# Masked row maximum in the first attention layer: TensorE mask only in score banks of two or four heads

## The chip, the cores and the metric

The kernel runs on one core of one Trainium2 chip. The metric is the device time of one execution in microseconds. Three runs of the kernel before gave 665.36, 666.23 and 666.69, so the median is 666.23 us.

## The reference

The input `x` is four sequences of 512 tokens and 256 channels. Six residual blocks follow each other, each on a layer norm of `x`:

```
x = x + 0.5 * ffn0(ln(x))     # dequantised weights, silu gate, hidden size 704
x = x + attn0(ln(x))          # 16 heads of 16, rotary embedding, causal
x = x + 0.5 * ffn0(ln(x))
x = x + 0.5 * ffn1(ln(x))     # ternary weights found from mean |w|, sigmoid gate
x = x + attn1(ln(x))          # 16 query heads, 4 key heads, linear bias, causal
x = x + 0.5 * ffn1(ln(x))
```

An attention layer computes, for each head, `softmax(q k^T / 4 + causal mask) v`. The softmax needs, for each query row, the maximum of the row's scores over the keys that the mask leaves. The change touches only how that maximum is found, and only in `attn0`.

## The kernel before

**Layout.** L is the layer pair (0 or 1), b the sequence (0 to 3). One attention `attn(L, b)` handles its 16 heads in four groups `g` of four heads. Queries and keys of a group lie in `Qs[g]` and `Ks[g]`, split into bf16 parts along the partitions, and reach these tiles over DRAM (`parts` writes, `fill` in L487 to L495 reads back, all on the SP queue).

**Pass 1** (`pass1`, L574 to L614) finds the row maxima of a group. Queries are taken in four chunks `c` of 128 rows; because of the causal mask, chunk `c` needs only the first `128*(c+1)` keys. A `unit` fills one PSUM bank of 512 columns (tag `s`, four buffers, shared with pass 2 and with a few FFN tiles): chunk 0 puts four heads of 128 keys into one bank, chunk 1 two heads of 256 keys (two units), and chunks 2 and 3 one head of 384 or 512 keys (four units each). This makes 11 units for each group, eight of them with one head. In the trace the bank of a unit is called `s_<g><c><first head>a`, so `s_132a` is group 1, chunk 3, head 2.

There are two forms of a unit. In the form called `summed`, used for L = 0 and b < 2, TensorE adds the mask into the bank with one more matmul, identity times a 128x128 mask block (L591), repeated for each head; then VectorE takes the maximum of all heads of the bank with one `tensor_reduce` (L593). In the other form, used everywhere else, no mask matmul runs; VectorE adds the mask and takes the maximum in one `tensor_tensor_reduce` for each head (L597), which the trace shows as two instructions, a CUSTOM_DVE_ANT_0 that writes the masked scores back into the bank, and a DVE_READ_ACCUMULATOR2_ANT that delivers the maximum to `mxt`.

`fin` (L601) then transposes `mxt` on TensorE (L605), splits the negated maxima into two bf16 rows on VectorE (L607, L608) and sends these to two rows of `Qs[g]` over SP (L610).

**Pass 2** (`pass2`, L618) computes the scores again in transposed form with the maxima already subtracted (L639), takes the exponential on ScalarE (L644), zeroes the masked corner on GpSimd (L646), and multiplies by the values (L659).

**Other work beside it.** The FFNs (`mtile` L369, `down` L421, activation parts L391 to L410), layer norms (L315 to L350), projections (L467, L565, L749), rotary embedding (L519 to L524). While the first two sequences are in `attn0`, the weights of `ffn1` are loaded in pieces over SP, summed as absolute values on ScalarE (L190, L201), turned into a threshold (`level`, L205 to L213) and quantised on VectorE (L229, L230).

**What sets the order.** Every piece of work is a function with a due time in `plan`, made from the tables `PLAN` and `MOVES` (a correction for single entries of the list, by their number); the pieces are issued in the order of due time (`plan.sort`, L818). The kernel is then built with `schedule_with_timeline_sim=True` (L907): the framework places each engine's instructions by its own estimate of how long they take, with the issued order as priority. The order on an engine is fixed when the kernel is built; every engine then works strictly through its own list.

Of the kernel before, what the change touches and what calls it, by code (L numbers as in the profile page):

```python
# [84 lines left out]
def macaron(ctx, tc, x, gu0, wd0, s0, sd0, wa0, wq1, wkv1, wo1, bo1, gu1, wd1,  # L85
# [365 lines left out]
    def attn(L, b, tag):  # L451
# [119 lines left out]
        def kst(g):  # L571
            return Ks[g] if L == 0 else Ks[b % 2]

        def pass1(g):  # L574

            Q, K = Qs[g], kst(g)

            summed = L == 0 and b < 2

            def unit(c, hs, N):  # L580
                def f():
                    mx = mxt[g % 2][:, 0:16].rearrange("p (h c) -> p h c", h=4)
                    p = psc.tile([128, T], F32, tag="s", name=f"s1_{g}{c}{hs[0]}{tag}")
                    st = N
                    n = len(hs)
                    for i, h in enumerate(hs):
                        PE.matmul(p[:, i * st:i * st + N], Q[0:mr, h, c * 128:(c + 1) * 128],  # L587
                                  K[0:mr, h, 0:N], start=i == 0 or not summed, stop=not summed)
                    if summed:
                        pm = p[:, 0:n * N].rearrange("p (h n) -> p h n", n=N)  # L590
                        PE.matmul(pm[:, :, N - 128:N], identb, mask[:, T - 128:T].unsqueeze(1).to_broadcast([128, n, 128]),  # L591
                                  start=False, stop=True)
                        V.tensor_reduce(mx[:, hs[0]:hs[0] + n, c], pm, AX.X, ALU.max)  # L593
                        return
                    for i, h in enumerate(hs):
                        pi = p[:, i * st:i * st + N]
                        V.tensor_tensor_reduce(pi, pi, mask[:, T - N:T], 1.0, FLOOR, ALU.add, ALU.max,  # L597
                                               mx[:, h, c:c + 1])
                return f

            def fin():  # L601


                pt = pmm.tile([128, T], F32, tag="mm", name=f"mt{g}{tag}")
                PE.transpose(pt[:, 0:128], mxt[g % 2], ident)  # L605
                mt = wrk.tile([16, 2, 128], BF, tag="mt", name=f"mts{g}{tag}", bufs=1)
                V.tensor_scalar(mt[:, 0], pt[0:16, 0:128], -1.0, None, ALU.mult)  # L607
                V.scalar_tensor_tensor(mt[:, 1], pt[0:16, 0:128], -1.0, mt[:, 0], ALU.mult, ALU.subtract)  # L608
                for l in range(2):
                    SY.dma_start(Q[mr + l:mr + l + 1], mt[:, l])  # L610

            us = [unit(0, (0, 1, 2, 3), 128), unit(1, (0, 1), 256), unit(1, (2, 3), 256)]
            us += [unit(c, (h,), 128 * (c + 1)) for c in (2, 3) for h in range(4)]
            return us, fin  # L614

# [143 lines left out]
        if quick:  # L759
            pre = [list(th) + [rope(1, "k")], [rope(0, "q"), vproj(0), vproj(1)]]  # L760
        return dict(pre=pre, fills=fills, pass1=pass1, pass2=pass2,
                    post=([ctr(0)] if tail else []) + [ctr(1), oproj(0), oproj(1)], dram=None if tail else (fetch, recip, norm))

# [147 lines left out]
```

## Time and profile before

| quantity | value |
|---|---|
| median of three runs | 666.23 us (665.36 to 666.69) |
| the profiled execution, whole | 665.67 us |
| its span in the trace | 663.9 us, so 1.77 us lie around it |
| TensorE clock granted, mean | 0.995 |
| busy: TensorE matmul, VectorE, ScalarE, GpSimd | 635.8, 525.1, 450.6, 386.4 us |
| mask matmuls of L591 | 88, from 72.4 to 185.6 us |
| `tensor_reduce` of L593 | from 72.9 us to the last start at 188.65 us |

All times in the trace are in microseconds from the start of the span. PE is TensorE's matmuls, PEld its weight loads, which run beside them, DVE is VectorE, ACT ScalarE, POOL GpSimd, SPq the queue of SyncE that issues the DMAs. A line of a timeline gives start, duration, engine, line of the code, operation, tile written and tiles read. Durations of neighbouring instructions on one engine overlap in the trace, because an engine starts an instruction before the last one has left its pipeline. What an instruction takes from its engine is therefore the distance from its start to the next start, and not its duration.

### The profile page before, as it was taken

The numbers are of one execution on the slowest core, as the hardware profiler recorded it, in microseconds if no ns is written. First come the engines' busy times: TensorE is split into PE (matmuls) and PEld (weight loads), VectorE is DVE, ScalarE is ACT, GpSimd is POOL, SyncE is SP. The second block draws the span as 40 slices with busy tenths as digits, with TensorE's granted clock in tenths as the row PEclk, the third lists the DMA queues.
The fourth block names the chain that finished last, engine by engine and source line by source line (L and its number), as shares of the span: only waits on it lengthen the run. The fifth ranks groups of instructions, "written<-read, shape, count | busy, mean of one in ns | idle before, by whom it ended". The sixth has DMA issues, their size and how long they took to land.

```text
span 663.9 us, 13241 instructions
## 1 busy us (share of the span) xinstructions
PE 635.8 (96%) x4405; PEld 430.4 (65%) x4405; DVE 525.1 (79%) x1515; ACT 450.6 (68%) x893; POOL 386.4 (58%) x648
## 2 busy tenths in 40 slices
PE   7898899999989999999999999999999999999996
PEld 5686666556635776657676766776575674566585
DVE  7789889789799987887778797787969778895344
ACT  3675658777758477785859678685948757757733
POOL 4655957667528765576547756488645544543511
PEclk8999999999999999999999999999999999999999
DMA  8204504326551322222221221111311232101000
GB/s 273 94 2 135 150 2 137 106 77 203 166 166 52 96 70 72 81 63 82 81 63 29 77 67 51 35 37 51 98 58 29 74 92 74 53 3 33 0 33 33
DMA packets 38290, 51.41 MB, mean 77 GB/s; under 512 B 10634, under 2 KB 28458, under 8 KB 38222
## 3 DMA queue, kind: packets, MB, share of 16 engines
q1 hardware_dynamic: 37646, 49.85, 24.8%
q10 hardware_dynamic: 576, 0.72, 0.4%
q8 instruction: 35, 0.57, 0.4%
q14 instruction: 33, 0.27, 0.1%
HBM read 34.12 MB, written 16.16 MB: 76 GB/s over the span
## 4 chain that ended last, share of the span: by engine, by line
PE 75%; DVE 8%; ACT 7%; POOL 6%; issue 2%; DMA 1%; ACTq 0%; DVEq 0%; POOLq 0%
PE pf L369 22%; PE df L421 11%; PE o0a L659 3%; PE o1a L659 3%; PE o3a L659 2%; PE o2a L659 2%; PE po0a L749 2%; PE po1a L749 2%; PE ltf L347 2%; ACT xnf L343 1%; POOL X L753 1%; PE pv1a L565 1%; POOL hlf L407 1%; PE pv0a L565 1%; PE paqa L467 1%
## 5 line engine op out<-in xcount | busy, mean ns | idle before, releaser
L369 PE MATMUL pf<-xhf,GU 128*128 128x512 f32 x352 | 123.6, 439 | 6.6 <-ACT xhf L349 2.8
L407 POOL TENSOR_TENSOR hlf<-hf,hhf 128x512 fp32r<-128x512 f32 x72 | 94.5, 1313 | 44.8 <-ACT hhf L406 44.1
L369 PE MATMUL pf<-xlf,GU 128*128 128x512 f32 x352 | 110.2, 401 | 0.0
L369 PEld LDWEIGHTS pf<-xhf,GU 128*128 128x128 f32 x352 | 60.8, 192 | 32.5 <-ACT xhf L349 4.9
L587 PEld LDWEIGHTS <-Qs 96*128 96x128 bf16 (+1 forms) x512 | 43.9, 98 | 53.8 <-issue 40.9
L369 PEld LDWEIGHTS pf<-xlf,GU 128*128 128x128 f32 x352 | 66.4, 190 | 15.5 <-DVE xlf L350 0.2
L639 PEld LDWEIGHTS <-Ks 98*128 98x128 bf16 (+1 forms) x512 | 43.2, 98 | 42.5 <-issue 30.3
L406 ACT CAST hhf<-hf 128x512 fp32r<-128x512 f32 x80 | 49.7, 621 | 22.1 <-DVE hf L404 15.6
L421 PE MATMUL df<-WD,hhf 128*128 128x256 f32 x320 | 53.8, 286 | 2.3 <-ACT hhf L406 2.2
L404 DVE SCALAR_TENSOR_TENSOR hf<-tf,pf 128x512 f32<-128x512 f32 (+1 forms) x48 | 32.9, 685 | 27.7 <-PE pf L369 18.1
L597 DVE DVE_READ_ACCUMULATOR2_ANT mxt<- 128x1 f32 x384 | 52.7, 137 | 0.2
L421 PE MATMUL df<-WD,hlf 128*128 128x256 f32 x320 | 50.9, 285 | 0.0
L421 PEld LDWEIGHTS df<-WD,hhf 128*128 128x128 f32 x320 | 44.4, 188 | 4.6 <-ACT hhf L406 3.8
L399 POOL TENSOR_TENSOR hf<-tf,hf 128x512 f32<-128x512 f32 x30 | 39.5, 1315 | 10.5 <-DVE tf L396 5.4
L343 ACT ACTIVATE xnf<-X,mrf,rsf 128x256 f32<-128x256 f32 x60 | 31.8, 593 | 18.2 <-POOL mrf L323 10.7
L421 PEld LDWEIGHTS df<-WD,hlf 128*128 128x128 f32 x320 | 43.2, 189 | 0.5
L403 ACT ACTIVATE tf<-pf 128x512 f32<-128x512 f32 (+1 forms) x48 | 28.1, 595 | 14.2 <-PE pf L369 14.0
L646 POOL TENSOR_SCALAR_AFFINE_SELECT Ks<-Ks 128x128 f32<-128x128 f32 (+2 forms) x54 | 19.3, 357 | 25.9 <-ACT Ks L644 25.3
L395 ACT ACTIVATE tf<-pf,sgh 128x512 f32<-128x512 f32 (+1 forms) x36 | 24.9, 691 | 7.0 <-PE pf L369 6.6
L349 ACT CAST xhf<-ltf 128x512 fp32r<-128x512 f32 x32 | 18.4, 591 | 15.4 <-PE ltf L347 15.0
L396 DVE SCALAR_TENSOR_TENSOR tf<-tf,pf 128x512 f32<-128x512 f32 (+1 forms) x36 | 24.4, 679 | 5.1 <-ACT tf L395 4.8
L315 DVE BATCH_NORM_STATS2 bsf<-X 128x6 f32<-128x256 f32 x64 | 23.6, 413 | 3.5 <-POOL X L426 2.3
(700 smaller groups left out, 2042.5 us busy)
## 6 DMA issues: line engine op xcount, KB each, us to landing
Qs<-drqa SPq DMA_DIRECT2D x96, 128.0 KB
Ks<-drka SPq DMA_DIRECT2D x60, 128.0 KB
out_dram<-X SPq DMA_DIRECT2D x8, 256.0 KB
droa<-oT0a SPq DMA_DIRECT2D x7, 256.0 KB
droa<-oT1a SPq DMA_DIRECT2D x7, 256.0 KB
cna<-droa SPq DMA_DIRECT2D x7, 256.0 KB
X<-in_x_dram SPq DMA_DIRECT2D x3, 512.0 KB
drka<-raka SPq DMA_DIRECT2D x4, 384.0 KB
```

The costliest lines, as they stand in the source:

```text
L343: S.activation(xn[c], X[b][:, c], AF.Identity, bias=mr[:, i:i + 1], scale=rs[:, i:i + 1])
L369: PE.matmul(p, w[:, m:m + 128], xx[:, k], start=n == 0, stop=n == 3)
L399: G.tensor_tensor(h, t, h, ALU.mult)
L403: S.activation(t, g, AF.Tanh, scale=0.5)
L404: V.scalar_tensor_tensor(h, t, 1.0, u, ALU.add, ALU.mult)
L406: S.copy(hh, h)
L407: (V if big and i % 2 or (first or last and big) and i > 2 else G).tensor_tensor(hl, h, hh.bitcast(F32), ALU.subtract)
L421: PE.matmul(p[:, cc], ho[l, i][:, ts], WD[L][:, i], start=n == 0, stop=n == 10)
L587: PE.matmul(p[:, i * st:i * st + N], Q[0:mr, h, c * 128:(c + 1) * 128], K[0:mr, h, 0:N], start=i == 0 or not summed, stop=not summed)
L597: V.tensor_tensor_reduce(pi, pi, mask[:, T - N:T], 1.0, FLOOR, ALU.add, ALU.max, mx[:, h, c:c + 1])
L639: PE.matmul(p[:, i * N:i * N + N], K[0:nr, h, kc * 128:(kc + 1) * 128], Q[0:nr, h, kc * 128:T], start=True, stop=not steep(h))
L659: m = PE.matmul(o[0][32 * h:32 * h + 32, kc * 128:T], va[:, kc, hv * VS:hv * VS + 32], pt[kc, h], start=kc == 0, stop=kc == 3)
```

## The change

`summed` is no longer decided once for the attention, but for each unit, and the condition gains `c < 2`. For L = 0 and b < 2, the units of chunks 0 and 1 (four and two heads in the bank) keep the mask matmul and the common `tensor_reduce`; the units of chunks 2 and 3 (one head) take the other form. With eight such units in each of four groups of two sequences, 64 units change. Plan, due times and everything else stay as they are.

```diff
             Q, K = Qs[g], kst(g)
 
-            summed = L == 0 and b < 2
 
             def unit(c, hs, N):
+
+                summed = L == 0 and b < 2 and c < 2
+
                 def f():
                     mx = mxt[g % 2][:, 0:16].rearrange("p (h c) -> p h c", h=4)
```

## The prediction

> **What bounds the kernel now.** I read the page first, for the busy shares and the chain that ended last; then the busy time of each engine in windows over the stretch that the change touches (72 to 206 us); then the timelines of TensorE and VectorE there, start to start; last the waits.
>
> The page:
>
> ```profile
> span 663.9 us, 13241 instructions
> PE 635.8 (96%) x4405; PEld 430.4 (65%) x4405; DVE 525.1 (79%) x1515; ACT 450.6 (68%) x893; POOL 386.4 (58%) x648
> PE 75%; DVE 8%; ACT 7%; POOL 6%; issue 2%; DMA 1%; ACTq 0%; DVEq 0%; POOLq 0%
> ```
>
> TensorE is busy nearly always and holds three quarters of the chain; VectorE is second in both. So work taken from TensorE shortens the run wherever VectorE has room. The windows (columns: window, length, busy time and count of PE, PEld, DVE, ACT, POOL, then clock, DMA share, GB/s):
>
> ```profile
> 72.00:80.00 8.00, 7.97 (x58) 5.64 (x57) 7.13 (x13) 6.01 (x11) 7.84 (x11) 1.00 0.51 154
> 80.00:88.00 8.00, 7.49 (x60) 6.09 (x58) 7.09 (x15) 2.19 (x4) 4.13 (x4) 1.00 0.01 1
> 95.00:112.00 17.00, 17.00 (x125) 11.17 (x123) 16.57 (x29) 14.37 (x29) 13.09 (x20) 1.00 0.29 96
> 112.00:126.00 14.00, 13.88 (x99) 7.88 (x98) 9.05 (x18) 10.77 (x22) 10.38 (x18) 1.00 0.42 131
> 126.00:148.00 22.00, 21.90 (x158) 12.20 (x157) 18.52 (x33) 16.24 (x35) 13.24 (x27) 1.00 0.25 73
> 178.00:190.00 12.00, 10.11 (x82) 4.96 (x82) 11.86 (x30) 9.35 (x19) 5.38 (x14) 1.00 0.56 169
> ```
>
> Three kinds of stage are to be seen. From 72 to 88 VectorE sets the pace: in its timeline it runs from 72.87 to 86.0 without a gap, and GpSimd is full to 80. From 95 to 148 TensorE is full; VectorE is nearly full too up to 112 and has room after that. From 178 to 190 VectorE is full with quantising the ffn1 weights, while TensorE has 1.9 us idle. The timeline places the 64 units so: 16 from 73 to 88, 8 from 95 to 106, 8 from 107 to 121, 16 from 126 to 149, 8 from 155 to 173, 8 from 177 to 186.
>
> **What is removed: 64 mask matmuls on TensorE.** The record of one is 219 ns (L591, 128 columns), but its price is the start-to-start distance. The TensorE timeline, with two kinds of follower:
>
> ```profile
> 87.36 0.39 PE L587 MATMUL s_132a<-Ks,Qs 96*128 96x512 bf16 x1
> 87.59 0.22 PE L591 MATMUL s_132a<-mask,identb 128*128 128x128 bf16 x1
> 87.65 0.38 PE L587 MATMUL s_133a<-Ks,Qs 96*128 96x512 bf16 x1
> ...
> 105.40 0.22 PE L591 MATMUL s_233a<-mask,identb 128*128 128x128 bf16 x1
> 105.43 0.71 PE L369 MATMUL pf<-xhf,GU 128*128 128x512 f32 x2
> 105.98 0.63 PE L369 MATMUL pf<-xlf,GU 128*128 128x512 f32 x2
> ...
> 109.50 0.62 PE L369 MATMUL pf<-xhf,GU 128*128 128x512 f32 x2
> 109.96 0.63 PE L369 MATMUL pf<-xlf,GU 128*128 128x512 f32 x2
> ```
>
> Before another score matmul the mask takes 0.06 us (87.59 to 87.65). Before an fp32 matmul it takes 0.03, and the follower is then held back by its own 190 ns weight load: the pair at 105.43 takes 0.55 to its successor, the undisturbed pair at 109.50 takes 0.46, so 0.03 + 0.09 = 0.12. Eleven of the 64 are followed by an fp32 matmul of pf, df, po or paqa, the other 53 I put at 0.06 (some show more, up to 0.15 before the value product, where a wait lies in the distance). 53 x 0.06 + 11 x 0.12 = 3.2 + 1.3 = 4.5 us of TensorE, 0.07 for one unit.
>
> **What is replaced on VectorE: 64 reduces by 64 pairs.** The durations suggest a large loss: 546 ns (384 columns) and 679 ns (512) against 556 + 137 and 730 + 137. The VectorE timeline says otherwise:
>
> ```profile
> 76.66 0.68 DVE L593 TENSOR_REDUCE mxt<-s_030a 128x1 f32<-128x512 f32 x1
> 77.26 0.68 DVE L593 TENSOR_REDUCE mxt<-s_031a 128x1 f32<-128x512 f32 x1
> ...
> 205.16 0.73 DVE L597 CUSTOM_DVE_ANT_0 s_032a<-s_032a,mask 128x512 f32<-128x512 f32 x1
> 205.81 0.14 DVE L597 DVE_READ_ACCUMULATOR2_ANT mxt<- 128x1 f32 x1
> 205.81 0.68 DVE L396 SCALAR_TENSOR_TENSOR tf<-tf,pf 128x512 f32<-128x512 f32 x1
> 206.41 0.69 DVE L597 CUSTOM_DVE_ANT_0 s_033a<-s_033a,mask 128x512 f32<-128x512 f32 x1
> 207.01 0.14 DVE L597 DVE_READ_ACCUMULATOR2_ANT mxt<- 128x1 f32 x1
> ```
>
> A reduce holds VectorE 0.60 us. The masked maximum holds it 0.60 (206.41 to 207.01) when another kind of operation went before, and 0.65 (205.16 to 205.81) when an accumulator read did; the read starts together with what follows it and adds nothing more. Over the whole trace, wherever no wait comes between, the medians are 0.47 and 0.60 for the reduce, 0.48 and 0.61 for the pair, 0.515 and 0.65 after a read. So 0.01 to 0.05 more for one unit. I take 0.03, the middle, since runs of one-head units and mixed places are about equally common: 64 x 0.03 = 1.9 us (0.6 to 3.2).
>
> A rule of the Trainium skill speaks against this: "VectorE: DVE Perf Modes", section Rules for kernel authors, says to minimise the count of operations, since each pays its own pipeline drain. By it the 0.14 us of each read would be added whole, some 9 us of VectorE as an estimate, and the change would lose. The start-to-start rows above don't show that cost.
>
> **Waits and queues.** No DMA is added or moved, on SP or on any other queue. The VectorE instruction no longer waits for the mask matmul, so it may start 0.06 earlier. The bank is written back and comes free later: the CUSTOM lasts 0.69 to 0.73 against 0.68, and if the read's end counted it would be 0.14 more, so 0.01 to 0.19 per bank. In the stretch TensorE waited for a bank held by L593 four times, 0.2 to 0.3 each; four waits longer by these bounds cost 0.04 to 0.8 us, and behind such a wait stands everything else on TensorE's list. I take 0.2, near the row of the CUSTOM, which is the one that uses the bank. The last maximum of a group, which L605 and the SP transfers of L610 wait for, comes later by at most the same 0.19; behind L610 on SP stand the fills of L495 and the weight pieces of L190 and L221. That lies inside the same bound and I count it once.
>
> **The sum by stage.** From 72 to 88: TensorE's 16 x 0.07 = 1.1 us falls into waits for VectorE and GpSimd, so I count none of it; VectorE's 16 x 0.03 = 0.5 is partly swallowed by its gaps of 0.2 and 0.7 us at 86 and 87, so 0.2, and the bank waits lie here, 0.2 more: +0.4 (bounds -1.1 and +1.3). From 95 to 106: both are full, 8 x 0.07 = 0.56 on one side and nothing or 0.24 on the other, I take half: -0.3. From 107 to 121: -0.56. From 126 to 149: 16 x 0.07 = -1.1. From 155 to 173: -0.5, TensorE holds most of the chain there. From 177 to 186: VectorE holds the chain, 8 x 0.03: +0.2, and TensorE's saving falls into its idle time. Together -1.9, say -2 us. After 190 the code is the same and TensorE holds most of the chain, so the lead is carried to the end. The SP transfers of the ffn1 weights in between wait for buffers that the engines free and not for a clock of their own, so they move with the lead.
>
> One term has no row: the framework places instructions by its own estimates, so that 64 other instructions can change the order on every engine from 72 us on. The nearest row is the largest hole of TensorE here, 2.79 us idle between 185 and 195 (7.21 busy of 10); one such hole more or fewer bounds it at +2.8 and -2.8, two at +5.6. I take 0 in the sum, because the trace favours neither sign, and leave it to the range.
>
> The profiled execution took 665.67, so 663.7 by its own measure; it lies 0.56 under the median of 666.23. Against the median the forecast is 664.2 us, 0.3% faster.
>
> **The rivals.**
> *Another order costs more than is saved (slower).* One new hole of the size seen at 185 to 195, in a stretch where TensorE is full, less the 2 us: +0.8; two: +3.6, 669.8. It decides from one hole of 2 us upward. For it: units sit between FFN and pass 2 matmuls at fine grain (s_020a comes after s_032a at 77.44), so the order is open to small shifts. Against it: the two forms of the unit take the same time on VectorE, and the later sequences already run in the new form at 100% TensorE (245 to 265: 20.00 of 20.00). About 668.5.
> *VectorE pays the durations (slower).* If a pair costs 0.15 to 0.19 more, as durations say, 36 of the units stand where VectorE is full (16 + 8 before 106, about 4 up to 112, 8 after 177): 36 x 0.17 = 6.1, less 28 x 0.07 = 2.0: +4.1, 670.3. It decides from 0.06 a unit. Against it stand the start-to-start rows.
> *TensorE's saving is lost (no change).* The lead could end at 178 to 193, where the chain runs through VectorE and a weight DMA of 4.2 us, if that DMA is held by its own data: 666.2. The Trainium skill, "Trainium Kernel Development and Optimization", section Performance Expectations, calls matmul busy time a bad measure and the share of weight loads a good one; by that the 65% of PEld would leave TensorE room, and the sum would be near 0. The 95 to 148 rows show no gap, with fp32 matmuls back to back.
> *TensorE sets the pace everywhere.* All 4.5 us come out: 661.7. Against it, VectorE at 72 to 88 and 178 to 190.
>
> **How the numbers follow.** A measurement of this kernel tells about 0.2% (1.3 us) from no change. Chances: the forecast 0.32 (its own range 662.5 to 664.8), all of the saving 0.10, so faster 0.42; lost 0.18, the same; another order 0.30 and VectorE's durations 0.10, so slower 0.40. The range from 661 to 670.5 reaches from the full saving with a little over it to two holes and the durations' case; about 1 in 10 is left out at each end.
>
> **What would show it.** Right: mask matmuls 24 instead of 88; TensorE's busy time between 95 and 149 lower, the last L597 unit of b = 1 and the start of ffn1's quantising earlier by 1 to 2 us; the pair at 0.47 to 0.52 and 0.60 to 0.65 start to start between 72 and 190; the stage 72 to 88 as long as before or 0.4 longer. Wrong: VectorE's waits for banks grow, TensorE shows new idle stretches of over 1 us after 72, or the order of units against pf and df matmuls differs and the loss comes after 190, where no code changed.

## The result

The changed kernel takes 668.57 us (median of five, 668.08 to 669.07) beside 665.9 us for the kernel before: ratio 1.0033, 95% interval 1.0018 to 1.0049. A second measurement of the changed kernel gave 667.71 us and 1.0018 (1.0006 to 1.003). So it is slower by 0.2 to 0.3%, 1.2 to 2.2 us. The ratios here and below are those on record, with their intervals; they are not the quotients of the medians, which can lie 0.1% beside them (here 1.0040). The profiled execution took 668.57 us itself.

The page after:

```profile
span 666.6 us, 13180 instructions
PE 633.9 (95%) x4341; PEld 425.7 (64%) x4341; DVE 529.8 (79%) x1579; ACT 451.6 (68%) x893; POOL 386.4 (58%) x648
PE 73%; DVE 9%; ACT 7%; DMA 4%; POOL 4%; issue 2%; SPq 1%; ACTq 0%; DVEq 0%; POOLq 0%
```

The work did what was meant: TensorE has 64 matmuls fewer and is busy 1.9 us less, VectorE has 64 instructions more. The span is 2.7 us longer all the same. In the chain, DMA rose from 1 to 4% and TensorE fell from 75 to 73%. The windows (columns: window, length, busy time and count of PE, PEld, DVE, ACT, POOL, then clock, DMA share, GB/s):

```profile
72.00:80.00 8.00, 7.45 (x44) 4.75 (x43) 6.25 (x18) 6.58 (x12) 7.84 (x10) 1.00 0.65 184
80.00:88.00 8.00, 7.26 (x54) 5.88 (x53) 8.00 (x23) 2.37 (x5) 4.22 (x5) 1.00 0.00 0
95.00:112.00 17.00, 16.62 (x115) 10.57 (x114) 16.15 (x37) 13.93 (x29) 13.59 (x21) 1.00 0.24 77
112.00:126.00 14.00, 12.88 (x76) 6.98 (x74) 10.66 (x25) 10.18 (x20) 10.36 (x17) 1.00 0.44 145
126.00:148.00 22.00, 21.39 (x159) 11.51 (x157) 18.31 (x45) 16.04 (x35) 12.50 (x25) 1.00 0.27 78
178.00:190.00 12.00, 8.70 (x70) 3.85 (x69) 11.46 (x37) 9.62 (x22) 5.16 (x14) 1.00 0.47 145
```

TensorE, which was full from 95 to 148, now stands still for 0.38, 1.12 and 0.61 us in its three windows there, where it has 1.9 us less to do. This execution was already 1.14 us behind that of before at 60 to 72 us, where the code and the order are the same, so the fixed windows cover slightly different work. A better ruler is the start of the same TensorE instruction in both traces, the later one less the earlier one, less the value at 60 to 72 us; I call its median over a stretch the lag. For the changed kernel it is -0.22 us at 100 to 110, +0.89 at 114 to 121, +0.44 at 149 to 155, and +2.52 at 212 to 230; from there it falls slowly, to 1.6 at the end. So 1.1 us are lost in a few microseconds near 112, and about 2 more between 155 and 212, shortly before the point (216 us) from which both kernels run the same instructions in the same order.

Why there? When I compared the two programs, they did not only differ in the 64 units. Each engine's list is in another order too: between 77 and 216 us 54 instructions of TensorE stand at another place among the others, 38 of VectorE, 22 of ScalarE, 14 of GpSimd and 12 DMAs of SyncE. Before 77 us and after 216 us the lists agree. Here is one such difference, first before (start, duration, engine, line, operation):

```profile
110.64 0.69 DVE L410 TENSOR_TENSOR h5f<-hf,h5f 64x512 fp32r<-64x512 f32 x1
111.36 0.56 DVE L593 TENSOR_REDUCE mxt<-s_321a 128x1 f32<-128x384 f32 x1
...
111.50 1.17 POOL L484 TENSOR_TENSOR rcqa<-rq2a,rcqa 128x512 bf16<-128x512 f32 x1 [1.44 <-ACT rcqa L483]
112.62 0.30 POOL L646 TENSOR_SCALAR_AFFINE_SELECT P102a<-P102a 128x128 f32<-128x128 f32 x1
```

and then in the changed kernel (its lines from the unit on are numbered two higher):

```profile
111.94 0.57 DVE L599 CUSTOM_DVE_ANT_0 s_321a<-s_321a,mask 128x384 f32<-128x384 f32 x1 [0.35 <-PE s_321a L589]
...
112.60 1.50 DVE L410 TENSOR_TENSOR h5f<-hf,h5f 64x512 fp32r<-64x512 f32 x1
114.13 0.69 DVE L595 TENSOR_REDUCE mxt<-s_300a 128x4 f32<-128x512 f32 x1
...
112.39 1.17 POOL L484 TENSOR_TENSOR rcqa<-rq2a,rcqa 128x512 bf16<-128x512 f32 x1 [1.35 <-ACT rcqa L483]
113.51 0.75 POOL L648 TENSOR_SCALAR_AFFINE_SELECT P102a<-P102a 128x128 f32<-128x128 f32 x1
...
114.88 0.32 PE L589 MATMUL s_322a<-Ks,Qs 96*128 96x384 bf16 x1 [0.78 <-DVE mxt L595]
```

Two VectorE instructions have changed places. VectorE first waits 0.35 us for the bank s_321a, and `h5f` (the low part of an FFN activation) then starts just behind GpSimd's `rcqa` instead of ahead of it. The same instruction takes 1.50 us in place of 0.69, until GpSimd's is over; GpSimd's next one is drawn out too, from 0.30 to 0.75. The maximum of s_300a comes late, and TensorE waits 0.78 us for its bank, with the whole list behind. This is a *collision*: two instructions, neither of them changed, that happen to meet, so that one waits for the other.

### The profile page after: what moved, and what is told of

The parts are those of the page before. It is cut to its first block, busy times and chain, and to the rows that moved or that the text cites. A ratio compares the mean times of both kernels' runs of the same rounds, so it can differ in the third digit from the quotient of the medians.

```text
span 666.6 us, 13180 instructions
## 1 busy us (share of the span) xinstructions
PE 633.9 (95%) x4341; PEld 425.7 (64%) x4341; DVE 529.8 (79%) x1579; ACT 451.6 (68%) x893; POOL 386.4 (58%) x648
## 4 chain that ended last, share of the span: by engine, by line
PE 73%; DVE 9%; ACT 7%; DMA 4%; POOL 4%; issue 2%; SPq 1%; ACTq 0%; DVEq 0%; POOLq 0%
PE pf L369 20%; PE df L421 11%; PE o1a L661 3%; PE o3a L661 3%; PE o0a L661 2%; PE o2a L661 2%; PE po0a L751 2%; PE po1a L751 2%; PE ltf L347 1%; ACT xnf L343 1%; DMA ws<-in_gu_dram 1%; DMA wa0s<-in_wa_dram 1%; PE pv1a L565 1%; DVE tf L396 1%; PE pq1a L467 1%
## 5 line engine op out<-in xcount | busy, mean ns | idle before, releaser
L369 PE MATMUL pf<-xhf,GU 128*128 128x512 f32 x352 | 122.0, 433 | 7.1 <-ACT xhf L349 2.5
L599 DVE DVE_READ_ACCUMULATOR2_ANT mxt<- 128x1 f32 x448 | 62.2, 139 | 0.2
L398 ACT ACTIVATE hf<-pf,sgu 128x512 f32<-128x512 f32 x30 | 20.8, 694 | 9.2 <-PE pf L369 5.2
```

What stands on the lines that cost most here:

```text
L369: PE.matmul(p, w[:, m:m + 128], xx[:, k], start=n == 0, stop=n == 3)
```

## The experiments

**How an order is held fixed.** A kernel was built in which the framework may not choose: after all pieces are issued, each engine's instructions are chained by edges that cost no semaphore, in an order read from a table (`ORDER`).

```diff
+    marks = []
     for _, f in plan:
+        marks.append(len(nc.cur_bb.bb.instructions))
         f()
+    in_order(tc, nc, marks)
...
+def in_order(tc, nc, marks):
...
+    info = mybir.DependencyInfo(mybir.DependencyClass.NoSync, mybir.DependencyReason.SCHED_ONLY)
...
+            if last is not None:
+                tc.add_manual_dep(i, last.name, info, reason="order")
+            last = i
```

With before's instructions and before's own order this gives instruction for instruction the program of before, and with the changed kernel's instructions and order that of the changed kernel; so what is measured below is the order and not the edges. All kernels below but the last one have this edit; their further edit is shown with each. They keep the line numbers of before.

**Instructions and order, taken apart.** *New instructions, old order*: the change as in its diff, `ORDER` = before's. *Old instructions, new order*: before's `unit`, `ORDER` = the changed kernel's, each removed mask matmul put right behind its score matmul.

> The instructions of the changed kernel, but each engine's list held in the order that the kernel before has. Theory 'order' (the changed instructions save what the forecast said, and the loss comes from the new order on the engines): about 2 us under the kernel before, 663 to 665 us, and the mask matmuls 24 in number. Theory 'VectorE pays' (the masked maximum costs VectorE more than the reduce, so the order is beside the point): as slow as the changed kernel, 667.5 to 669.5. Theory 'start' (over 1 us of the loss is already there before 72 us, where no code changed): this run is at most 1 us away from the changed kernel less what the stretch after 72 us gave, so 667.

> The instructions of the kernel before (mask matmul and reduce in every bank of the first two sequences), in the order that the changed kernel has; each mask matmul stands right behind its score matmul. Theory 'order': slower than both, the changed kernel's 668.6 plus the 2 to 4.5 us that the mask matmuls take, 670 to 673. Theory 'VectorE pays': the order costs nothing, 665 to 667.

Measured: new instructions in the old order 666.04 beside 666.68 us, ratio **0.9982 (0.997 to 0.9994)**; old instructions in the new order 669.89 us, ratio **1.0056 (1.0037 to 1.0074)**. (The medians alone would give 0.9990 and 1.0048. The theory 'order' had expected 663 to 665 and 670 to 673 us, so both effects came out somewhat smaller than it said.) The instructions by themselves make the kernel faster by 0.18%, 1.2 us (0.4 to 2.0 by the interval). The new order by itself, with not one instruction changed, makes it slower. With the new instructions the order costs 1.0018 - 0.9982 = 0.36% to 1.0033 - 0.9982 = 0.51%, 2.4 to 3.4 us, each of these ratios being known to 0.1 or 0.2%. The intervals of the two orders do not overlap, so the sign is settled: the change is a small gain, and the other order that came with it takes more than that away.

**The two halves of the change, in the old order.** *VectorE's part alone* keeps all mask matmuls and takes the masked maximum in the one-head banks; *TensorE's part alone* leaves those mask matmuls out and keeps the plain reduce.

```diff
 vector_part_alone
-                        V.tensor_reduce(mx[:, hs[0]:hs[0] + n, c], pm, AX.X, ALU.max)
-                        return
+                        if c < 2:
+                            V.tensor_reduce(mx[:, hs[0]:hs[0] + n, c], pm, AX.X, ALU.max); return
 tensor_part_alone
-                                  K[0:mr, h, 0:N], start=i == 0 or not summed, stop=not summed)
+                                  K[0:mr, h, 0:N], start=i == 0 or not summed, stop=not (summed and c < 2))
...
-                        PE.matmul(pm[:, :, N - 128:N], identb, mask[:, T - 128:T]...
+                        if c < 2: PE.matmul(pm[:, :, N - 128:N], identb, mask[:, T - 128:T]...
```

> Order of the kernel before, mask matmuls kept in all banks, and in the one-head banks the masked maximum on VectorE in place of the reduce (the mask is then added twice, which leaves the maximum as it is). It prices the VectorE half of the change alone. Forecast: 64 pairs at 0.01 to 0.05 us more, of which the stages with a full VectorE pay some 0.4 to 1 us: 666.3 to 667. Theory 'VectorE pays': 36 of the 64 at 0.17 us, 671 to 673.

> Order of the kernel before, no mask matmul in the one-head banks, and the plain reduce kept, so the mask is left out of the row maxima of those banks. It prices the TensorE half of the change alone: at most 64 x 0.07 = 4.5 us, by stages about 2.5 us: 663 to 664. If TensorE's saving is lost at the quantising stage around 180 us: 665.5 to 666.5.

Measured: VectorE's part 1.0000 (0.9991 to 1.001), TensorE's part 0.9989 (0.9976 to 1.0002). The pairs on VectorE cost nothing that can be measured; the saving on TensorE is worth about 0.7 us alone and 1.2 us in the whole, the same within the intervals. TensorE's part had been forecast at 663 to 664 us and took 665.35. So of 4.5 us taken off TensorE about a quarter reaches the end (a tenth to under a half by the interval of the whole).

**Where the order costs.** The two orders consist of blocks that can be exchanged at points where every engine has done the same set of instructions. *To 125*: the changed kernel's order up to about 125 us, before's from there. *To 178* and *from 178*: the same cut at about 178 us, and its complement. *One swap back*: the changed kernel's order, and on VectorE only

```diff
 VectorE's list near 112 us
-s_321a<-s_321a,mask
 h5f<-hf,h5f
+s_321a<-s_321a,mask
```

> The changed kernel's instructions; up to about 125 us (the plan's entries up to number 160) each engine's list is in the changed kernel's order, and after that in the order of the kernel before. The theory (two separate losses: 1.0 us at 112 to 115 us, where h5f<-hf,h5f on VectorE comes beside GpSimd's rcqa and takes 1.50 us instead of 0.69, and about 2.5 us between 150 and 212 us) expects the old order's 0.9982 plus 1.0 us, so about 0.9997, with h5f<-hf,h5f near 113 us at about 1.5 us. The rival (one loss, behind the transfer of wq at 191 to 196 us and the quantising around it; whatever is lost earlier would be waited for there anyway) expects 0.998 as in the old order.

> As the run before, but the changed kernel's order goes up to about 178 us (the plan's entries up to number 250, as far as the first norm of the next tiles), and the old order holds from there. The theory expects the old order's 0.9982 plus 1.0 us plus what the lag gains between 150 and 178 us in the changed kernel (0.6 us), so 1.0003 to 1.0008. The rival expects 0.998 still, since the quantising of the gate and up weights, the transfer of wq and the down weights behind it are in the old order.

> The complement of the run before: old order up to about 178 us, the changed kernel's order from there on. The theory expects 0.9982 plus what the lag gains after 178 us in the changed kernel (about 1.9 us), so about 1.001. The rival (all of the loss sits there) expects 1.0033, as the changed kernel.

> The changed kernel's instructions in the changed kernel's order throughout, but for one pair on VectorE near 112 us: h5f<-hf,h5f goes again ahead of the masked maximum of s_321a, as in the kernel before. If the collision with GpSimd's rcqa there costs what the trace shows (1.50 us instead of 0.69, and 0.35 us of waiting for s_321a ahead of it), h5f takes 0.7 us again and the time falls by 0.8 to 1.0 us against the changed kernel: about 1.0020. If that microsecond is lost again further on, it stays at 1.0033.

Measured: to 125 1.0015 (1.0 to 1.003); to 178 0.9995 (0.9984 to 1.0005); from 178 1.0017 (1.0004 to 1.0029); one swap back 1.001 (1.0 to 1.002). The rival's single late loss would have left the first two at 0.998 and put the third at 1.0033. The intervals of "to 125" and "from 178" lie above that of the old order (0.997 to 0.9994), so an early and a late part of the order each cost something. The ratios are not finer than about 0.1%, though: "to 178" contains all of "to 125" and came out lower, with an interval that overlaps that of the old order. Of the theory's own figures, 0.9997 for "to 125" lies outside what was measured, and the others lie in their intervals or at the edge. What happens near 112 us is better seen in the traces (lag in us):

| kernel | order near 112 us | `h5f` takes | lag at 100 to 110 | at 114 to 121 | at 149 to 155 |
|---|---|---|---|---|---|
| changed | new | 1.50 | -0.22 | +0.89 | +0.44 |
| changed, again | new | 1.50 | -0.23 | +0.79 | +0.18 |
| to 125 | new | 1.51 | -0.18 | +0.86 | +0.30 |
| to 178 | new | 1.51 | -0.19 | +0.84 | +0.47 |
| late swaps back | new | 1.50 | -0.23 | +0.84 | +0.53 |
| old instructions, new order | new | 1.44 | +0.21 | +1.23 | +1.23 |
| new instructions, old order | old | 0.68 | -0.37 | -0.32 | -0.90 |
| from 178 | old | 0.69 | -0.38 | -0.32 | -0.62 |
| one swap back | one pair old | 0.68 | -0.20 | -0.18 | -0.47 |

Every trace with the new order there gains 1.0 to 1.1 us of lag from 100-110 to 114-121, and no other gains more than 0.1. Putting one pair of VectorE instructions back removes it, and the difference is still there at 149 to 155: -0.5 against +0.2 to +0.5. Further on it is less sure. At 170 to 178 us the four traces with the new instructions in the changed kernel's order lie at -0.03 to +0.42, and the three with the pair put back (one swap back, and the kernels *both swaps back* and *three back* below) at -0.10, -0.90 and -0.96, though these three have the same lists up to 196 us; and "to 125", which goes on in the old order from there, has made its loss good by then (-0.47). So that the pair costs 1 us at 112 us is shown, and what of it reaches the end is not. In the trace of one swap back:

```profile
111.19 0.68 DVE L410 TENSOR_TENSOR h5f<-hf,h5f 64x512 fp32r<-64x512 f32 x1 [0.24 <-ACT h5f L409]
111.91 0.57 DVE L597 CUSTOM_DVE_ANT_0 s_321a<-s_321a,mask 128x384 f32<-128x384 f32 x1
...
111.75 1.17 POOL L484 TENSOR_TENSOR rcqa<-rq2a,rcqa 128x512 bf16<-128x512 f32 x1 [1.35 <-ACT rcqa L483]
```

`h5f` is ahead of `rcqa` again, and the maximum that now runs beside `rcqa`, with its scores in PSUM, is not slowed: 0.57 us in both places.

**The late stretch.** The changed kernel shows three more collisions there, with the last weights of the down projection:

```profile
200.24 1.28 DVE L229 TENSOR_SCALAR WD<-wq,thr 128x512 fp32r<-128x512 f32 x1
...
202.78 1.38 DVE L410 TENSOR_TENSOR h5f<-hf,h5f 64x512 fp32r<-64x512 f32 x1
...
205.54 1.32 DVE L230 SCALAR_TENSOR_TENSOR WD<-wq,thr,WD 128x512 fp32r<-128x512 f32 x1
...
199.54 1.70 POOL L399 TENSOR_TENSOR hf<-tf,hf 128x512 f32<-128x512 f32 x1 [1.50 <-DVE tf L396]
...
202.35 1.27 POOL L407 TENSOR_TENSOR hlf<-hf,hhf 128x512 fp32r<-128x512 f32 x1
...
205.03 1.28 POOL L399 TENSOR_TENSOR hf<-tf,hf 128x512 f32<-128x512 f32 x1 [1.41 <-DVE tf L396]
```

A smaller one stands ahead of them: `GU` (L229) at 187.44 us takes 0.82 instead of 0.40 beside an affine select of GpSimd. Before has none of the three on VectorE. Where the two engines meet there, VectorE is first and GpSimd pays (its `hf` takes 1.73 instead of 1.28, behind the L230 of 199.14):

```profile
199.14 0.75 DVE L230 SCALAR_TENSOR_TENSOR WD<-wq,thr,WD 128x512 fp32r<-128x512 f32 x1
...
200.80 0.79 DVE L230 SCALAR_TENSOR_TENSOR WD<-wq,thr,WD 128x512 fp32r<-128x512 f32 x1
...
202.15 0.69 DVE L410 TENSOR_TENSOR h5f<-hf,h5f 64x512 fp32r<-64x512 f32 x1
...
199.31 1.73 POOL L399 TENSOR_TENSOR hf<-tf,hf 128x512 f32<-128x512 f32 x1 [0.62 <-DVE tf L396]
```

The kernel *late swaps back* puts VectorE's list between 196 and 207 us as before; *both swaps back* adds the swap near 112 us; *three back* also takes `h5f` two places later. (Twelve of the 15 places differ, not ten as the expectation has it.)

```diff
 VectorE's list, 196 to 207 us (late swaps back)
-s_000a, WD (L229), hf, s_012a, tf, WD (L230), s_000a, WD (L229), WD (L230), s_021a, h5f, tf, s_022a, rda, WD (L230)
+s_012a, WD (L229), s_000a, WD (L230), hf, WD (L229), tf, WD (L230), s_000a, s_021a, rda, WD (L230), s_022a, h5f, tf
 three back, in addition
-h5f, tf, s_023a
+tf, s_023a, h5f
```

> The changed kernel's instructions in the changed kernel's order, but for VectorE's list between about 196 and 207 us (15 instructions, ten of which differ in place: quantising of the last down weights, two evictions tf<-tf,pf, h5f<-hf,h5f, one reciprocal, three masked maxima), which is as in the kernel before. The theory says that a VectorE instruction with two operands in SBUF that starts while a GpSimd tensor_tensor runs waits for its end: in the changed kernel WD<-wq,thr takes 1.28 us instead of 0.55, h5f<-hf,h5f 1.38 instead of 0.69 and WD<-wq,thr,WD 1.32 instead of 0.79, together 1.95 us on an engine that is full from 196 to 212 us. With VectorE's old order there these should go, and the time should fall by up to 2.0 us, to about 1.0003; by some 0.7 to 1.0 us less if h5f<-hf,h5f meets another GpSimd instruction, as it does in two of the old-order runs. The rival (the order of the other engines, or the later start of the stretch, costs the time) expects 1.0033 as in the changed kernel.

> The edit of the run before and that of new_order_one_swap_back together: 17 places of VectorE's list are as in the kernel before, everything else (PE, ScalarE, GpSimd, SyncE and the rest of VectorE's list) in the changed kernel's order. The theory expects both gains: 1.0010 less 1.0 to 2.0 us, so 0.998 to 0.9995, near the 0.9982 of the whole old order. The rival expects no better than the 1.0010 of the one swap.

> As new_order_both_swaps_back, and h5f<-hf,h5f near 203 us goes two places later on VectorE, behind the eviction tf<-tf,pf and the masked maximum of s_023a, whose inputs lie ready by then; it should start when GpSimd's hlf<-hf,hhf is just over and take about 0.7 us instead of 1.67, and tf, for which GpSimd waited 1.40 us and TensorE 0.54 us, comes 1.7 us earlier. The theory expects 0.9999 less 0.8 to 1.2 us, so 0.998 to 0.9987, all that the old order brings. If the time stays at 0.9999, the rest of the order's cost is elsewhere.

> The changed kernel itself, unaltered, beside the run before, to narrow its own interval and to see its collisions in a second execution. Expected 1.0033 again (1.0018 to 1.0049), with h5f<-hf,h5f near 112 us at about 1.5 us and three VectorE instructions between 198 and 207 us at 1.2 to 1.4 us. If the collisions were an accident of the one profiled execution, they should be absent.

Measured: late swaps back 1.0015 (1.0002 to 1.0027); both swaps back 0.9999 (0.9985 to 1.0014); three back 1.0011 (1.0001 to 1.0022), a miss; changed again 1.0018 (1.0006 to 1.003), with `h5f` at 1.50 near 112 and the three late ones at 1.28, 1.39 and 1.31, so the collisions are no accident of one execution. In the two swap kernels both WD collisions are gone and `h5f` meets the next GpSimd instruction and takes 1.67 us. The window 206 to 212 shows what TensorE gets (before, changed, both swaps back; each from its own trace):

```profile
206.00:212.00 6.00, 5.91 (x49) 4.15 (x48) 5.50 (x24) 5.69 (x12) 5.11 (x8) 1.00 0.29 76
```

```profile
206.00:212.00 6.00, 4.02 (x24) 2.14 (x23) 5.97 (x19) 4.47 (x10) 6.00 (x10) 1.00 0.32 90
```

```profile
206.00:212.00 6.00, 5.30 (x46) 2.92 (x44) 5.31 (x21) 4.35 (x10) 6.00 (x10) 1.00 0.32 91
```

TensorE is busy 5.91, 4.02 and 5.30 of 6 us. With three collisions at a granted clock of 1.00 over the window it is 4.0 to 4.6 (changed, from 178, one swap back); with one it is 5.3 to 5.6 (late and both swaps back, and three kernels in the old order). Those three had a collision of `h5f` as well, of 1.74 to 1.76 us, so the old order is no guarantee; it depends on when the stretch is reached.

The miss, in its trace:

```profile
201.41 1.83 DVE L410 TENSOR_TENSOR h5f<-hf,h5f 64x512 fp32r<-64x512 f32 x1
...
201.40 1.29 POOL L399 TENSOR_TENSOR hf<-tf,hf 128x512 f32<-128x512 f32 x1
```

I had `h5f` start where GpSimd's `hlf` ends. It does, but the earlier `tf` had GpSimd's next instruction ready, which starts 0.01 us ahead of it, and `h5f` waits for all of that one. Its lag was -0.5 us at 186 to 190 us, as good as the old order, and +1.7 at 212 to 230; in that profiled execution TensorE's granted clock was 0.72 from 206 to 212 us:

```profile
206.00:212.00 6.00, 5.74 (x37) 3.67 (x37) 4.65 (x20) 3.94 (x8) 3.11 (x6) 0.72 0.31 94
```

So that trace mixes a collision with a lower clock. Seven of the profiled executions had a clock of 1.00 all through this stretch. In them the lag grows from 186-190 to 212-230 us by 1.9 and 1.3 us with three collisions (changed, from 178), and by 1.1, 0.9, 0.8, 0.7 and -0.2 us with one (late swaps back, both swaps back, TensorE's part, to 125, VectorE's part). The changed kernel and the two swap kernels differ from 155 us on in VectorE's list alone, so moving VectorE's instructions there was worth 0.8 to 1.0 us in these three traces. In the whole time that is not shown: the intervals of the changed kernel, one swap back, late swaps back, both and three overlap. The only version here that is faster than both kernels beyond its interval is the new instructions in the old order, 0.9982.

## Why the prediction was wrong

**The step that failed is the order term.** The prediction took 0 for it, "because the trace favours neither sign", and left it to the range. It measured 2.4 to 3.4 us (the whole changed kernel against its instructions in the old order), around the bound of one hole, 2.8. The prediction also said that no DMA is moved; twelve were. The time falls on the rival "Another order costs more than is saved", about 668.5. That the number fits is partly luck: the rival looked for one new hole in TensorE, and what came were several small waits on VectorE, 0.5 to 0.8 us each, one of them before 115 us. The price of such a wait could have been read in the trace of before, where the old order has some too:

```profile
106.55 1.38 DVE L482 TENSOR_TENSOR rq0a<-rq0a,raqa 128x512 f32<-128x512 f32 x1
...
106.10 1.27 POOL L524 TENSOR_TENSOR rq2a<-rq2a,rq3a 128x512 f32<-128x512 f32 x1
```

(`rq0a` takes 0.69 us as a rule.) And that trace did favour a sign in one place: from 190 to 212 us no VectorE instruction in it is held up by GpSimd. There another order could add collisions and take none away. Elsewhere some pass GpSimd's closely, as `h5f` does, which ends at 111.33, 0.2 us ahead of the start of `rcqa`. The list of what would show it wrong asked for a loss "after 190, where no code changed"; in the changed kernel's trace 1.9 us of lag came between 190 and 212, where the code is the same and the order is not, and 1.1 near 112.

**TensorE's saving came out smaller than its sum, as far as the runs can tell.** 4.5 us of work less is right in its parts: 24 mask matmuls are left, and in the old order the next bf16 matmul as a rule comes 0.06 us sooner where nothing waits. The stage sums gave -1.9, which the interval of the ratio (-0.4 to -2.0) just still holds. In the old order, free of the order's effect, the lag shows -0.30 at 88 to 95 us (predicted +0.4 for 72 to 88), -0.37 at 100 to 110 (another -0.07; predicted -0.3), -0.32 at 114 to 121 (+0.05; -0.56), -0.90 at 149 to 155 (-0.6; -1.1) and about -0.8 at 170 to 190 (+0.1; -0.3 for both stages together). That is -0.8 for -1.9, and the ratio says -1.2. The largest piece of what is missing, 0.8 us, belongs to 95 to 121 us, where TensorE looked full and yet the saving didn't come through. From 95 to 106, before and then with the new instructions in the old order:

```profile
95.00:106.00 11.00, 11.00 (x77) 7.04 (x75) 10.67 (x21) 8.76 (x18) 9.48 (x15) 1.00 0.16 57
```

```profile
95.00:106.00 11.00, 10.67 (x67) 6.49 (x66) 10.86 (x28) 9.01 (x18) 9.39 (x15) 1.00 0.21 74
```

TensorE, at 11.00 of 11, did not set the pace alone: with less to do it idles 0.33 us, and VectorE goes from 10.67 to 10.86. The prediction allowed for that here by half; for 107 to 121 us it took TensorE's busy share as the bound. Why 107 to 121 and 155 to 186 us gained nothing is not settled.

**VectorE's term was right.** 0.03 us for one unit, 1.9 in all, mostly out of the way: VectorE's part alone measured 1.0000. Start to start the pair takes what the prediction read from the rows of before; after:

```profile
121.29 0.14 DVE L599 DVE_READ_ACCUMULATOR2_ANT mxt<- 128x1 f32 x1
121.29 0.73 DVE L599 CUSTOM_DVE_ANT_0 s_331a<-s_331a,mask 128x512 f32<-128x512 f32 x1
121.94 0.14 DVE L599 DVE_READ_ACCUMULATOR2_ANT mxt<- 128x1 f32 x1
121.94 0.73 DVE L599 CUSTOM_DVE_ANT_0 s_332a<-s_332a,mask 128x512 f32<-128x512 f32 x1
```

0.65 us from one to the next, with the read inside. So the rival "VectorE pays the durations" (670.3) falls. The rule of the Trainium skill that the prediction weighed there ("VectorE: DVE Perf Modes", section Rules for kernel authors), by which it estimated some 9 us more of VectorE, is not borne out for this read. *TensorE's saving is lost* and *TensorE sets the pace everywhere* (661.7) fall by the -1.2 of the old order: neither none nor all of it arrives.

**The bank waits were mis-sized.** The prediction priced four waits of TensorE for VectorE's maxima at +0.2 us. Counting its waits of over 0.15 us between 72 and 191 us that end with `mxt`, the trace of before has 4, together 0.86 us; with the new instructions in the old order there are 10, together 2.57 us. VectorE's part alone has 8 (1.67 us), TensorE's part alone 5 (1.42 us). Here are some of them, before and then with the new instructions in the old order:

```profile
81.44 0.32 PE L587 MATMUL s_122a<-Ks,Qs 96*128 96x384 bf16 x1 [0.22 <-DVE mxt L593]
82.04 0.32 PE L587 MATMUL s_123a<-Ks,Qs 96*128 96x384 bf16 x1 [0.22 <-DVE mxt L593]
```

```profile
78.02 0.38 PE L587 MATMUL s_100a<-Ks,Qs 96*128 96x128 bf16 x4 [0.27 <-DVE mxt L597]
80.94 0.32 PE L587 MATMUL s_121a<-Ks,Qs 96*128 96x384 bf16 x1 [0.23 <-DVE mxt L593]
81.54 0.32 PE L587 MATMUL s_122a<-Ks,Qs 96*128 96x384 bf16 x1 [0.27 <-DVE mxt L593]
82.14 0.32 PE L587 MATMUL s_123a<-Ks,Qs 96*128 96x384 bf16 x1 [0.28 <-DVE mxt L593]
```

So 1.7 of the 4.5 us went into waits for VectorE, in later stages as well as in the first. Either half of the change alone lengthens them; how much comes from maxima that are ready later and how much from TensorE being there sooner was not separated. The first stage still came out 0.1 to 0.3 us shorter, and not 0.4 longer, with the new instructions in either order.

## What to carry to other kernels

Where a framework fixes the order of each engine's list by its own estimates, a change of some instructions is two changes. Compare the lists of both kernels first, and measure the new instructions in the old order before judging them; here the verdict turned from 0.18% faster to 0.2 to 0.3% slower. Look for instructions on two engines that just miss each other, since another order can make them meet; and don't read a full engine as the bound while another beside it is nearly full too.

## What was not expected of the hardware

**VectorE and GpSimd shut each other out.** In these traces a VectorE instruction whose operands all lie in SBUF and which starts while GpSimd runs a tensor_tensor ends only 0.3 to 0.6 us after that one has: `h5f` takes 0.69 us alone, 1.38 to 1.83 behind one; WD (L229) 0.48 and 1.28; WD (L230) 0.75 and 1.32. The other way, GpSimd's `hf` takes 1.28 alone and 1.70 to 1.73 behind a VectorE instruction, an affine select 0.30 and 0.75. VectorE instructions that read PSUM (`tf<-tf,pf` 0.67 to 0.69, the masked maximum 0.69 to 0.75 at 512 columns) kept their time beside GpSimd. The Trainium skill has the rule: "Trainium Architecture — The Big Picture", section What this means for kernel authors, says that the port pair that VectorE and GpSimd share is an exclusive lock and not a split of bandwidth, and "GPSIMD Engine Reference", section Specifications, names VectorE instructions with two inputs in SBUF, or in a two-port performance mode, as those that contend. The rows agree with both, but don't tell which of the two applies to L229, whose inputs are one tensor and a column of scalars. Read against the two timelines of before, the rule would have shown where another order can hurt.

**The granted clock falls in one stretch.** From 72 to 178 us TensorE's granted clock is 1.00 in all fourteen profiled executions here; between 178 and 214 us it is below 1 in seven of them, down to 0.68 over 12 us, at places that differ. The windows hide what it is: the clock is at one half for 3.41 us, or for two or three times that, and at 1.00 otherwise. In before:

```profile
195.91:199.32 3.41, 3.41 (x10) 1.62 (x8) 3.35 (x10) 2.07 (x5) 0.59 (x3) 0.50 0.01 1
```

The other six executions have it at 180.7 and 204.6 (changed, again), 193.9 (6.8 us, new instructions in the old order), 187.5 (10.2 us, old instructions in the new order), 197.0 (6.8 us, to 178), 179.7 (one swap back) and 207.0 (three back); the changed kernel's own has none. As an estimate from this, 3.41 us at half clock take at most 1.7 us of TensorE's work. What sets it off was not tried. It makes lags past 178 us uncertain by 1 to 2 us, and since before has such a piece itself, all lags past 199 us are measured against a trace that lost some time there. The whole times show it too: of the executions of before, those with a mean clock of 1.000 took 665.7 us on average (18 of them) and those with 0.992 took 667.6 (11), a spread as large as the effects measured here.

**The start differs.** At 60 to 72 us, where all programs are the same, the profiled executions lie between 0.41 us ahead of that of before and 1.70 behind it. A comparison of two traces by fixed times carries that with it.
